# Window sums in two PSUM banks by turns, and the window's share of the first layer copied two octets ahead

## The chip, the cores and the metric

The kernel runs on one core of one Trainium2 chip. The metric is device time in microseconds (us), the median of several executions. A core has five engines that run side by side, each with its own queue of instructions: TensorE (PE in the profile; PEld is its weight load), VectorE (DVE), ScalarE (ACT), GpSimd (POOL), and SyncE (SP), which issues transfers (DMAs). They wait for each other through semaphores only. Matmul results land in PSUM, which has eight banks per partition; a bank holds 512 float32 values.

## What is computed

One layer of a graph network over 12,500 nodes with 64 features and 400,000 edges, which come sorted by `dst`, followed by a residual and a layer norm:

```python
m_in = concatenate([x[src], x[dst], edge_attr], axis=-1)      # 64 + 64 + 16
h = silu(m_in @ W1 + b1)
messages = silu(h @ W2 + b2)
agg = segment_sum(messages, dst, num_segments=12500)
z = silu(concatenate([x, agg], axis=-1) @ W3 + b3)
out = layernorm(x + z)
```

All of it is float32. Call the three 64- or 16-row parts of `W1` W1a (for `x[src]`), W1b (for `x[dst]`) and W1c (for the edge's own attributes).

## The kernel before, in words

**Tiling.** Edges are taken 128 at a time (a tile) and eight tiles make an octet: 1,024 edges. There are 391 octets (`NO`). The body of the loop over `o` (lines 610 to 681) is written out by hand for PE, ScalarE, VectorE and SyncE: `tc.manual_schedule` (line 607) keeps each engine's instructions in the order of the text. GpSimd's queue holds gathers only and runs ahead on its own.

**x[src].** At the start ScalarE writes `x @ W1a` to a table `pa` in memory (`table`, octets 1 to 7). The first 12 octets (`RAW`) gather rows of `x` itself, which TensorE transposes (line 454) and multiplies by W1a. From octet 12 on, GpSimd's `gather` (line 373) fetches the rows `pa[src]` of an octet with one indirect transfer per tile, into one of five buffers `ga`; a buffer is free again when TensorE's matmuls of line 463 have read it. Two or four tiles of some octets are not gathered: ScalarE and VectorE together move 136 columns of `x` an octet (36 and 32 each, `columns`, lines 295 to 309), one 4-byte column per instruction and at an address that a register holds, and SyncE fetches 16 rows an octet (`rows`, line 333). So most octets have eight or six gathers.

**x[dst].** As the edges are sorted, an octet's destinations lie in a window of 48 nodes (`S`). `window_load(o)` (SyncE, line 401) fetches the 48 rows of `x` twice over into `xr`; `window_product(o)` (TensorE, line 406) multiplies them by W1b into a PSUM tile of the pool `mis`; `window_copy(o)` (VectorE, line 411) multiplies that by a mask and puts it into `xw[o % 3]`, above the rows of W1c. `compare_dst(o)` (VectorE, line 433) makes the one-hot matrix `oh` that picks each edge's window row.

**An octet through the engines.** `first_layer(o)`: line 450 multiplies `xw` by `oh` into the PSUM tile `p1`; lines 460 and 463 add the columns' and the gathered parts; ScalarE moves its 36 columns and then does the silu of line 467 into `h`. `second_layer(o)`: lines 476 and 478 make `p2`, ScalarE moves its 32 columns and does the silu of line 482 into `m`. `add_up(o)` (line 491) multiplies `m` by the one-hot matrix `eh` (VectorE, line 439), which gives the sums of the window's 48 nodes; `add_window(o)` (VectorE, line 496) adds them into `agg` at an address from a register. The sums of four octets share one PSUM tile, and so one bank (`sums`, line 371).

**The order within iteration o** (what the change touches):

- TensorE: `window_product(o + 1)`, `first_layer(o)`, `add_up(o - 2)`, `second_layer(o - 1)`, then what `todo` holds.
- VectorE: `add_window(o - 4)`, `compare_dst(o + 1)`, 36 columns, `window_copy(o + 1)`, `compare_nodes(o + 1)`, 32 columns, then addresses and what `todo` holds.
- ScalarE: 36 columns, silu of `first_layer(o)`, 32 columns, silu of `second_layer(o - 1)`.
- SyncE: the transfers of octets ahead, `window_load(o + 3)`, and last the 16 rows.

**Nodes.** When no more edges can reach a group of 512 nodes, `todo` puts its output work into the loop: `node_product` (TensorE, lines 523 to 526, reads `agg`), a silu (ScalarE, line 532), and the layer norm on VectorE. Of 25 groups 23 come within the loop, one about every 16 octets; the last two come at its end.

**PSUM.** Eight banks: two for `mis` (window products, the tables, the raw octets' transposes, the node products), one for constants (`wps`), two each for `p1` and `p2`, one for the sums.

Of the kernel before, what the change touches and what calls it, by code (L numbers as in the profile page):

```python
# [9 lines left out]
F32 = mybir.dt.float32  # L10
# [4 lines left out]
OP = mybir.AluOpType  # L15
AX = mybir.AxisListType
PSUM = bass.MemoryType.PSUM
DRAM = bass.MemoryType.DRAM
ENG = mybir.EngineType

P = 128
G = 4
CT = 24
OT = 8
S = 48
# [72 lines left out]
def windows(ctx, tc, ident, badi, pa, x, xt, src_c, src_row, dst_c, dst_row, attr_t, dst_2, attr_2, base, w1, b1, w2, b2, w3, b3, out, edges):  # L98
    nc = tc.nc
# [69 lines left out]
    zero = const.tile([P, 1], F32, name="zero")  # L169
    nc.vector.memset(zero, 0.0)  # L170

    mis = ctx.enter_context(tc.tile_pool(name="mis", bufs=2, space=PSUM))


    def table(c):
        n = min(8 * P, N - c)
        ps = mis.tile([P, 8, D], F32, name="mm")
        k = (n + P - 1) // P
        for i in range(k):
            o = c + i * P  # L180
            nc.tensor.matmul(ps[:, i, :], xs[0:D, o:o + P], w1ab[:, 0, :], start=True, stop=True)
        j = c // (8 * P) % RB
        t = v[:, 2 * j:2 * j + 2].rearrange("p a i d -> p (a i) d")
        nc.scalar.copy(t[:, :k], ps[:, :k])
        f = n // P
        if f:
            nc.scalar.dma_start(pa[c:c + f * P, :].rearrange("(i p) d -> p i d", p=P), t[:, :f])
        if n % P:
            nc.scalar.dma_start(pa[c + f * P:c + n, :], t[:n % P, f, :])
# [43 lines left out]
    w1bb = fast.tile([D, 2, D], F32, name="w1bb")  # L233
    nc.vector.tensor_copy(w1bb, w1ab[:, 1:2, :].to_broadcast([D, 2, D]))
    xw = []
    for k in range(3):
        t = fast.tile([P, P], F32, name=f"xw{k}")
        nc.vector.memset(t, 0.0)
        for q in range(2):
            nc.sync.dma_start(t[E + q * A:E + (q + 1) * A, q * D:(q + 1) * D], w1[2 * D:2 * D + A, :])  # L240
        xw.append(t)
# [6 lines left out]
    with tc.tile_pool(name="gat", bufs=AHEAD + 2) as gat, tc.tile_pool(name="drp", bufs=2) as drp, \  # L248
# [2 lines left out]
            tc.tile_pool(name="work", bufs=2) as work, tc.tile_pool(name="win", bufs=3) as win, \  # L251
            tc.tile_pool(name="ps1", bufs=2, space=PSUM) as ps1, \
            tc.tile_pool(name="ps2", bufs=2, space=PSUM) as ps2, \
            tc.tile_pool(name="psa", bufs=1, space=PSUM) as psa, \
            tc.tile_pool(name="cx", bufs=4) as cx, tc.tile_pool(name="cxi", bufs=3) as cxi, \
            tc.tile_pool(name="rx", bufs=2) as rx, tc.tile_pool(name="rxi", bufs=2) as rxi, \
            tc.tile_pool(name="nx", bufs=2) as nx, tc.tile_pool(name="nv", bufs=1) as nv:
# [110 lines left out]
                    nc.vector.tensor_scalar(t[:, h], t[:, h], 4.0, float(XBASE[s] + XADDR), op0=OP.mult, op1=OP.add)  # L368

        winrow, winreg = {}, {}  # L370
        sums = psa.tile([P, 4, S], F32, name="pg")

        def gather(o):
            c, t0, n, first, last = octs[o]
# [12 lines left out]
        def bases(eng, o):  # L387

            n = min(4, NO - o)
            _, regs = nc.values_load_multi_w_load_instructions(  # L390
                bi[0:1, o:o + n], engines=(eng,), min_val=0, max_val=N - 1,
                skip_runtime_bounds_check_because="dst names a node")
            for i in range(n):
                winreg[eng, o + i] = regs[i]

        def window_load(o):
            if o % 4 == 0:
                bases(ENG.SP, o)
            xr = win.tile([D, 2, S], F32, name="xr")
            frm = xt[:, ds(winreg.pop((ENG.SP, o)), S)]  # L400
            nc.sync.dma_start(xr, frm[:, None, :].to_broadcast([D, 2, S]))
            winrow[o] = xr

        def window_product(o):
            pw = mis.tile([P, P], F32, name="mm")
            nc.tensor.matmul(pw[:E, :], winrow[o].rearrange("k s w -> k (s w)"), w1bb.rearrange("k s m -> k (s m)"),  # L406
                             start=True, stop=True)
            winrow[o] = pw

        def window_copy(o):  # L410
            nc.vector.tensor_tensor(xw[o % 3][:E, :], winrow.pop(o)[:E, :], mask[:E, :], op=OP.mult)  # L411

        def load(c, o0=0, o1=CT // OT):

# [28 lines left out]
        def first_layer(o):  # L443
            c, t0, n, first, last = octs[o]
            n2 = n + n % 2
            k = n2 // 2
            ga = got.pop(o)
            oh, eh = hots.pop(o)
            p1 = ps1.tile([P, OT // 2, P], F32, name="p1")
            nc.tensor.matmul(p1[:, :k], xw[o % 3], oh, start=True, stop=False, skip_group_check=True)  # L450
            if o < RAW:
                pt = mis.tile([P, OT // 2, P], F32, name="mm")
                for i in range(k):
                    nc.tensor.matmul(pt[:, i, :], ga[:, 2 * i:2 * i + 2, :].rearrange("p s d -> p (s d)"), ident,
                                     start=True, stop=True)
                xg = work.tile([P, OT // 2, P], F32, name="m")
                nc.vector.tensor_copy(xg[:, :k], pt[:, :k])
                nc.tensor.matmul(p1[:, :k], w1d, xg[:, :k], start=False, stop=True, skip_group_check=True)
            if o in pairs:
                nc.tensor.matmul(p1[:, 0, :], w1d, cols.pop(o), start=False, stop=False, skip_group_check=True)  # L460
            for i in range(1 if o in pairs else 0, k if o >= RAW else 0):
                g2 = single.pop(o) if o in rpairs and i == 1 else ga[:, 2 * i:2 * i + 2, :]
                nc.tensor.matmul(p1[:, i, :], g2.rearrange("p s d -> p (s d)"), ident,  # L463
                                 start=False, stop=(i == k - 1), skip_group_check=True)
            columns(o, ENG.Activation, 0)
            h = work.tile([P, OT // 2, P], F32, name="h")
            nc.scalar.activation(h[:, :k], p1[:, :k], AF.Silu, bias=b1s)  # L467
            made[o] = h, eh

        def second_layer(o):  # L470
            c, t0, n, first, last = octs[o]
            n2 = n + n % 2
            k = n2 // 2
            h, eh = made.pop(o)
            p2 = ps2.tile([P, OT, D], F32, name="p2")
            nc.tensor.matmul(p2[:, :n2, :], one3, b2r[:, :n2, :], start=True, stop=False, skip_group_check=True)  # L476
            for i in range(k):
                nc.tensor.matmul(p2[:, 2 * i:2 * i + 2, :].rearrange("p s d -> p (s d)"), h[:, i, :], w2d,  # L478
                                 start=False, stop=(i == k - 1), skip_group_check=True)
            columns(o + 1, ENG.Activation, 1)  # L480
            m = work.tile([P, OT, D], F32, name="m")
            nc.scalar.activation(m[:, :n2], p2[:, :n2], AF.Silu)  # L482
            made[o] = m, eh

        def add_up(o):
            c, t0, n, first, last = octs[o]
            m, eh = made.pop(o)
            pg = sums[:, o % 4, :]
            for i in range(n):
                s = i % 2  # L490
                nc.tensor.matmul(pg[s * D:(s + 1) * D, :], m[:, i, :], eh[:, i, :],  # L491
                                 start=(i < 2), stop=(i >= n - 2), skip_group_check=True)

        def add_window(o):
            a = agg[:, ds(winreg.pop((ENG.DVE, o)), S)]
            nc.vector.tensor_tensor(a, a, sums[:, o % 4, :], op=OP.add)  # L496


        groups = [(c, min(G * P, N - c)) for c in range(0, N, G * P)]
# [16 lines left out]
        def node_product(q):  # L516
            c, n = groups[q]
            p = n // G
            assert p * G == n
            po = mis.tile([P, G, D], F32, name="mm")  # L520
            av = agg[:, c:c + n].rearrange("k (p i) -> k i p", i=G)
            xv = xs[0:D, c:c + n].rearrange("k (p i) -> k i p", i=G)
            nc.tensor.matmul(po[:p], ones[:, :p], b3r, start=True, stop=False, skip_group_check=True)  # L523
            for i in range(G):
                nc.tensor.matmul(po[:p, i, :], xv[:, i], w3x, start=False, stop=False, skip_group_check=True)  # L525
                nc.tensor.matmul(po[:p, i, :], av[:, i], w3s, start=False, stop=(i == G - 1), skip_group_check=True)  # L526
            nodes[q].append(po)
# [62 lines left out]

        for o in range(min(AHEAD, NO)):
            gather(o)
        window_load(0)
        window_product(0)
        window_copy(0)
        load(0, 0, 1)
        load(0, 1, 3)
        window_load(1)
        window_load(2)
        relative(0, CT)  # L600
        lims = nv.tile([P, 2, LP], F32, name="lims")
        tables = list(range(0, N, 8 * P))
# [4 lines left out]
        with tc.manual_schedule(engines={ENG.PE, ENG.Activation, ENG.DVE, ENG.SP}):  # L607
            compare_dst(0)
            compare_nodes(0)
            for o in range(NO + 1):  # L610
# [27 lines left out]
                    gather(o + AHEAD)  # L638
                if o + 2 < NO and octs[o + 2][3] and o + 2:
                    load(octs[o + 2][0])  # L640
                if o + 3 < NO:
                    window_load(o + 3)
                if o + 1 < NO:
                    window_product(o + 1)
                if o % 4 == 2:
                    bases(ENG.DVE, o - 2)
                if o >= 4:
                    add_window(o - 4)
                if o + 1 < NO:
                    compare_dst(o + 1)  # L650
                columns(o, ENG.DVE, 0)
# [1 line left out]
                    first_layer(o)  # L653
                if o == 0:
                    nc.vector.tensor_copy(b2r, b2p[:, None, :].to_broadcast([3, OT, D]))
                if o + 1 < NO:
                    window_copy(o + 1)
                    compare_nodes(o + 1)
                columns(o, ENG.DVE, 1)
                if o == 1:  # L660
# [12 lines left out]
                    add_up(o - 2)  # L673
                if o >= 1:
                    second_layer(o - 1)
                address(o + 2)
                raddress(o + 2)
                rows(o)
# [21 lines left out]
        nc.vector.tensor_copy(badi, bs)  # L700

        add_up(NO - 1)
        for o in range(NO - 3, NO):
            add_window(o)
        for f, a in todo.get(NO, []):
            f(*a)
# [267 lines left out]
```

## Time and profile before

| | us |
|---|---|
| median of 3 runs (5423.18 to 5434.05) | 5430.6 |
| the profiled execution, one of the three | 5434.05 |
| its span, first to last instruction | 5432.3 |
| GpSimd, 2,585 gathers of line 382: busy | 2442.4 |
| ScalarE, 25,500 column copies of line 309: busy | 2739.9 |
| VectorE, 25,444 column copies of line 307: busy | 2071.9 |
| TensorE: matmuls busy | 2910.2 |
| first matmul of line 450 in octet 12 | 219.34 |
| first matmul of line 450 in octet 390 (the last) | 5404.21 |

So the loop takes 5185 us from octet 12 to octet 390, 13.7 us an octet. Busy time is the union of an engine's instructions; the copies overlap each other in the pipeline, so that 8 copies of 0.15 us each take 0.62 us. "Idle before" a group is how long its engine did nothing just ahead of it, and the name behind the arrow is what ended that: another engine's instruction, a DMA, or "issue" when the profile shows nothing that was waited for.

### The profile page before, as it was taken

What the parts mean: (1) busy time and instruction counts of PE and PEld (TensorE: products, weight loads), DVE (VectorE), ACT (ScalarE), POOL (GpSimd) and SP (SyncE); (2) the same over time, 40 slices, a digit from 0 to 9 for tenths busy, and PEclk for the clock granted to TensorE, in tenths of its full rate; (3) what the DMA queues carried; (4) which work ended last, traced back from release to release, by engine and by line L of the source; (5) the groups of instructions that cost most, each with busy time, mean ns of one, the idle gap of its engine ahead of it and who ended that gap; (6) DMA issues with size and microseconds to landing.
All of it is one profiled execution on the core that took longest, in us unless ns stands there. A gap on an engine that the chain in (4) does not pass through costs nothing. (4 is left out here: it accounts for less than half of the span.)

```text
span 5432.3 us, 114104 instructions
## 1 busy us (share of the span) xinstructions
PE 2910.2 (54%) x15131; PEld 2055.6 (38%) x15131; DVE 2796.6 (51%) x27841; ACT 3234.0 (60%) x26342; POOL 2535.3 (47%) x2690
## 2 busy tenths in 40 slices
PE   5654555555555455554554555555545455455556
PEld 3433333333333344333333333333433334333334
DVE  1355555555555555555555555555555555555554
ACT  1265666566565665666666656666666566666665
POOL 5544444444444444444444444444444444444443
PEclk7665656666656656666666656666566666666666
DMA  4321112111211121112112111111211121121121
GB/s 92 73 43 37 38 38 43 39 37 38 44 40 41 38 44 38 38 39 42 39 38 47 40 38 42 41 38 38 45 37 38 42 45 38 38 44 37 38 44 39
DMA packets 202940, 229.30 MB, mean 42 GB/s; under 512 B 133085, under 2 KB 141478, under 8 KB 201270
## 3 DMA queue, kind: packets, MB, share of 16 engines
q1 hardware_dynamic: 101562, 122.63, 10.1%
q0 software_dynamic: 85792, 88.02, 8.5%
q10 hardware_dynamic: 14812, 11.26, 0.9%
q14 instruction: 646, 5.29, 0.3%
q8 instruction: 128, 2.10, 0.2%
HBM read 215.26 MB, written 6.40 MB: 41 GB/s over the span
## 5 line engine op out<-in xcount | busy, mean ns | idle before, releaser
L382 POOL DMA_INDIRECT ga<-pa,sc x2585 | 2442.4, 945 | 2784.2 <-PE p L463 2059.9
L309 ACT COPY cx<-xs 64x4 uint8 x25500 | 2739.9, 188 | 1416.2 <-issue 1363.4
L307 DVE TENSOR_REDUCE cx<-xs 64x4 uint8 x25444 | 2071.9, 148 | 1817.0 <-issue 1748.0
L450 PE MATMUL p<-oh,xw 128*128 128x512 f32 (+1 forms) x782 | 793.5, 1117 | 2034.9 <-DVE xw L411 1390.2
L450 PEld LDWEIGHTS p<-oh,xw 128*128 128x128 f32 x782 | 192.2, 305 | 2140.5 <-DVE xw L411 1455.1
L463 PEld LDWEIGHTS p<-ident,ga 128*128 128x128 f32 x2586 | 597.9, 323 | 181.5 <-issue 181.2
L478 PE MATMUL p<-w2d,h 128*128 128x128 f32 x3126 | 606.8, 353 | 1.1 <-issue 1.1
L463 PE MATMUL p<-ident,ga 128*128 128x128 f32 x2586 | 600.8, 405 | 0.0
L478 PEld LDWEIGHTS p<-w2d,h 128*128 128x128 f32 x3126 | 513.7, 249 | 125.2 <-issue 125.2
L482 ACT ACTIVATE m<-p 128x512 f32<-128x512 f32 x391 | 232.3, 594 | 500.7 <-remote 408.0
L491 PE MATMUL pg<-eh,m 128*64 128x48 f32 x6250 | 352.8, 271 | 304.8 <-DVE agg L496 166.4
L491 PEld LDWEIGHTS pg<-eh,m 128*64 128x64 f32 x6250 | 304.9, 184 | 398.0 <-issue 251.4
L467 ACT ACTIVATE h<-p,b1s 128x512 f32<-128x512 f32 x391 | 267.0, 683 | 195.3 <-remote 68.5
L411 DVE TENSOR_TENSOR xw<-mm,mask 96x128 f32<-96x128 f32 x391 | 110.8, 283 | 523.6 <-issue 481.3
L406 PE MATMUL mm<-w1bb,xr 64*96 64x128 f32 x782 | 234.5, 391 | 100.3 <-remote 44.9
L433 DVE TENSOR_TENSOR oh<-dr,wrow 96x512 f32<-96x512 int32 x391 | 263.4, 674 | 3.2 <-DMA dr<-in_dst 1.8
L439 DVE TENSOR_TENSOR eh<-wrow,dc 128x384 f32<-128x384 f32 x391 | 213.4, 546 | 47.4 <-issue 47.4
L460 PEld LDWEIGHTS p<-cx,w1d 128*128 128x128 f32 x398 | 132.1, 332 | 202.2 <-issue 202.2
L406 PEld LDWEIGHTS mm<-w1bb,xr 64*96 64x96 f32 x782 | 124.3, 208 | 169.3 <-issue 57.9
L476 PE MATMUL p<-b2r,one 3*128 3x512 bf16 x391 | 186.6, 477 | 0.0
L496 DVE TENSOR_TENSOR agg<-agg,pg 128x48 f32 x391 | 77.4, 198 | 111.0 <-remote 20.5
L460 PE MATMUL p<-cx,w1d 128*128 128x128 f32 x398 | 124.7, 416 | 0.0
(81 smaller groups left out, 778.6 us busy)
## 6 DMA issues: line engine op xcount, KB each, us to landing
rx<-pa SPq DMA_DIRECT2D x5888, 0.2 KB
dr<-in_dst SPq DMA_DIRECT2D x260, 288.0 KB
ga<-pa,sc POOLq DMA_INDIRECT x2585
oh<-in_attr SPq DMA_DIRECT2D x130, 192.0 KB
xr<-in_xt SPq DMA_DIRECT2D x391, 24.0 KB
xs<-in_xt ACTq DMA_DIRECT2D x12, 512.0 KB
cxi<-in_src_row SPq DMA_DIRECT2D x199, 1.0 KB
pa<-v ACTq DMA_DIRECT2D x12, 256.0 KB
```

Source lines behind the costliest of these rows:

```text
L307: nc.vector.tensor_reduce(to, frm[:, :, None], AX.X, OP.max)
L309: nc.scalar.copy(to, frm)
L382: nc.gpsimd.indirect_dma_start(out=ga[:, i, :], out_offset=None, in_=x if o < RAW else pa[:, :], in_offset=bass.IndirectOffsetOnAxis(ap=sc ...
L406: nc.tensor.matmul(pw[:E, :], winrow[o].rearrange("k s w -> k (s w)"), w1bb.rearrange("k s m -> k (s m)"), start=True, stop=True)
L433: nc.vector.tensor_tensor(oh[:E, :], dr[:, e:e + w], wn[:E, o:o + 1].to_broadcast([E, w]), op=OP.is_equal)
L450: nc.tensor.matmul(p1[:, :k], xw[o % 3], oh, start=True, stop=False, skip_group_check=True)
L460: nc.tensor.matmul(p1[:, 0, :], w1d, cols.pop(o), start=False, stop=False, skip_group_check=True)
L463: nc.tensor.matmul(p1[:, i, :], g2.rearrange("p s d -> p (s d)"), ident, start=False, stop=(i == k - 1), skip_group_check=True)
L467: nc.scalar.activation(h[:, :k], p1[:, :k], AF.Silu, bias=b1s)
L478: nc.tensor.matmul(p2[:, 2 * i:2 * i + 2, :].rearrange("p s d -> p (s d)"), h[:, i, :], w2d, start=False, stop=(i == k - 1), skip_group_ch ...
L482: nc.scalar.activation(m[:, :n2], p2[:, :n2], AF.Silu)
L491: nc.tensor.matmul(pg[s * D:(s + 1) * D, :], m[:, i, :], eh[:, i, :], start=(i < 2), stop=(i >= n - 2), skip_group_check=True)
```

## The change

- The window product is made three octets ahead and no longer at the head of the iteration but after the second layer's matmuls; its copy goes into one of four buffers `xw`, two octets ahead; the window's load is four octets ahead.
- The pool `mis` has one PSUM buffer in place of two. The tables and the node products use `p2`'s tiles, the raw octets' transposes `p1`'s.
- The sums of an octet have a PSUM tile of their own, in two banks by turns, and `add_window` follows three octets behind in place of four.
- Before the loop, four window loads, three products and two copies come ahead of the first octet's other loads.

```diff
-    mis = ctx.enter_context(tc.tile_pool(name="mis", bufs=2, space=PSUM))
+    mis = ctx.enter_context(tc.tile_pool(name="mis", bufs=1, space=PSUM))
...
-        ps = mis.tile([P, 8, D], F32, name="mm")
+        ps = ps2.tile([P, OT, D], F32, name="p2")
...
-            tc.tile_pool(name="psa", bufs=1, space=PSUM) as psa, \
+            tc.tile_pool(name="psa", bufs=2, space=PSUM) as psa, \
...
-            nc.vector.tensor_tensor(xw[o % 3][:E, :], winrow.pop(o)[:E, :], mask[:E, :], op=OP.mult)
+            nc.vector.tensor_tensor(xw[o % 4][:E, :], winrow.pop(o)[:E, :], mask[:E, :], op=OP.mult)
...
-                pt = mis.tile([P, OT // 2, P], F32, name="mm")
+                pt = ps1.tile([P, OT // 2, P], F32, name="p1")
...
-            pg = sums[:, o % 4, :]
+            pg = sums[o] = psa.tile([P, S], F32, name="pg")
...
-            po = mis.tile([P, G, D], F32, name="mm")
+            po = ps2.tile([P, OT, D], F32, name="p2")[:, :G]
...
-        window_load(0)
-        window_product(0)
-        window_copy(0)
+        for o in range(4):
+            window_load(o)
+        for o in range(2):
+            window_product(o)
+            window_copy(o)
+        window_product(2)
         load(0, 0, 1)
         load(0, 1, 3)
-        window_load(1)
-        window_load(2)
...
-                if o + 3 < NO:
-                    window_load(o + 3)
-                if o + 1 < NO:
-                    window_product(o + 1)
-                if o % 4 == 2:
-                    bases(ENG.DVE, o - 2)
-                if o >= 4:
-                    add_window(o - 4)
+                if o + 4 < NO:
+                    window_load(o + 4)
+                if o % 4 == 1:
+                    bases(ENG.DVE, o - 1)
+                if o >= 3:
+                    add_window(o - 3)
...
+                if o + 2 < NO:
+                    window_copy(o + 2)
                 if o + 1 < NO:
-                    window_copy(o + 1)
                     compare_nodes(o + 1)
...
                 if o >= 1:
                     second_layer(o - 1)
+                if o + 3 < NO:
+                    window_product(o + 3)
                 address(o + 2)
                 raddress(o + 2)
                 rows(o)
```

More of the change, by code (lines that the diff above doesn't have):

```diff
@@ L235, in windows @@
     xw = []
-    for k in range(3):
+    for k in range(4):
         t = fast.tile([P, P], F32, name=f"xw{k}")
@@ L370, in windows @@
         winrow, winreg = {}, {}
-        sums = psa.tile([P, 4, S], F32, name="pg")
+        sums = {}
         def gather(o):
@@ L449, in first_layer @@
             p1 = ps1.tile([P, OT // 2, P], F32, name="p1")
-            nc.tensor.matmul(p1[:, :k], xw[o % 3], oh, start=True, stop=False, skip_group_check=True)
+            nc.tensor.matmul(p1[:, :k], xw[o % 4], oh, start=True, stop=False, skip_group_check=True)
             if o < RAW:
-                pt = mis.tile([P, OT // 2, P], F32, name="mm")
+                pt = ps1.tile([P, OT // 2, P], F32, name="p1")
                 for i in range(k):
@@ L495, in add_window @@
             a = agg[:, ds(winreg.pop((ENG.DVE, o)), S)]
-            nc.vector.tensor_tensor(a, a, sums[:, o % 4, :], op=OP.add)
+            nc.vector.tensor_tensor(a, a, sums.pop(o), op=OP.add)
         groups = [(c, min(G * P, N - c)) for c in range(0, N, G * P)]
@@ L702, in windows @@
         add_up(NO - 1)
-        for o in range(NO - 3, NO):
+        for o in range(NO - 2, NO):
             add_window(o)
```

## The prediction, made before the result was known

> **What bounds the kernel now.** I first read the waits, longest first in total (who waited, for whom: us in total, times, longest).
>
> ```profile
> POOL ga L382 <- PE p L463: 2059.9, 361, 10.3
> DVE cx L307 <- issue: 1748.0, 3447, 5.1
> ...
> PE p L450 <- DVE xw L411: 1390.2, 234, 9.7
> ACT cx L309 <- issue: 1363.4, 2102, 5.7
> ...
> DVE xw L411 <- issue: 481.3, 226, 6.6
> ...
> PE pg L491 <- DVE agg L496: 166.4, 175, 7.7
> ```
>
> GpSimd waits for TensorE (a free `ga` buffer), TensorE waits for VectorE's mask copy L411 and, less, for its `agg` sum L496. VectorE waits for nobody: 2796.6 busy (page, part 1) plus 1748.0 and 481.3 of "issue" is 5026 of 5432 us, and all idle time before L496 is 111.0. So the queue of VectorE sets the pace, and the question is what its "issue" time is. For that I took the busy time in four neighbouring stretches of the middle of the run (each stretch's length, then busy us and instructions by engine, granted PE clock, DMA share, GB/s).
>
> ```profile
> core 0: us, PE busy (x) PEld busy (x) DVE busy (x) ACT busy (x) POOL busy (x), PEclk, DMA share, GB/s
> 2512.00:2521.00 9.00, 0.66 (x5) 0.33 (x3) 2.03 (x20) 2.25 (x14) 5.63 (x6) 0.71 0.13 26
> 2521.00:2529.00 8.00, 6.50 (x37) 4.59 (x37) 6.13 (x67) 7.71 (x70) 2.83 (x3) 0.69 0.48 112
> 2529.00:2534.00 5.00, 0.00 (x0) 0.00 (x0) 0.97 (x8) 1.36 (x9) 2.83 (x3) 0.54 0.18 34
> 2534.00:2542.00 8.00, 6.78 (x37) 4.73 (x37) 6.17 (x64) 7.87 (x71) 2.83 (x3) 0.65 0.06 12
> ```
>
> The chip runs in two modes: eight us in which VectorE does 64 to 67 instructions and ScalarE 70, then five to nine in which they do 8 to 20 and 9 to 14. The timeline shows the slow mode close by (start, length, engine, line; idle before).
>
> ```profile
> 2518.14 0.19 ACT L309 COPY cx<-xs 64x4 uint8 x1 [1.17 <-issue]
> 2518.15 0.15 DVE L307 TENSOR_REDUCE cx<-xs 64x4 uint8 x1 [1.25 <-issue]
> ...
> 2518.84 0.19 ACT L309 COPY cx<-xs 64x4 uint8 x1 [0.51 <-issue]
> 2518.85 0.15 DVE L307 TENSOR_REDUCE cx<-xs 64x4 uint8 x1 [0.55 <-issue]
> ...
> 2521.04 0.27 DVE L411 TENSOR_TENSOR xw<-mm,mask 96x128 f32<-96x128 f32 x1
> ...
> 2521.36 0.50 PEld L450 LDWEIGHTS p<-oh,xw 128*128 128x128 f32 x2 [8.91 <-DVE xw L411]
> ```
>
> Both engines start one or two instructions together about every 0.7 us; GpSimd's gathers go on. I call it a silence. From the starts of all instructions of PE, DVE, ACT and SP I worked out: 2,560 gaps over 0.45 us, 1857 us together, a third of the span. Silences belong to gathers. Of the bursts of eight (168, 9.7 us long) the first silence comes 4.2 us after the first gather, the last ends 1.6 us after the last, 6.4 us are silent; of the bursts of six (168, 7.2 us) the numbers are 4.3, 1.2 and 3.7. The idle time ahead of a burst (2 to 9 us) makes a microsecond of difference at most. So an octet is a ring: L411 ends; L450 starts (mean 0.9 us later); L463 ends 3.7 later; the burst starts 0.3 later; silence 4.2 later. VectorE has some 9.3 us of work an octet (2796.6 / 391 = 7.15 busy, and about 2.1 of register loads between eights of copies), so silence catches it just short of the next L411: the median has 6 copies left. L411 comes before the silence in 5% of the bursts, within it in 36%, after it in 59%. The mean octet (20 to 369) is 13.83 us = VectorE's work, plus silence, less what gets through in it (mean 5.6 copies and 0.7 other instructions).
>
> **The change part by part.**
>
> *Sums in two banks, add_window an octet earlier.* L491 no longer waits for L496 (166.4 us on TensorE). This is worth 0: TensorE stands idle 2034.9 us before L450 (part 5), which hides it. What is late next is `m`: L491 now starts 3.0 us (mean) after it, in 5% of octets under 1.2. L496 needs the sums of an octet ago, with a whole octet to spare; VectorE issues the same number of each kind of instruction. If ScalarE fell behind by the 3 us, TensorE's idle time would take it.
>
> *The copy two octets ahead.* L450 of octet o+1 needs the copy of the iteration before. But in the changed order L406 of octet o+3 stands right ahead of it in TensorE's queue, and with one buffer in `mis` L406 waits until L411 of iteration o has read the product before: the same L411 that L450 waits for now. The wait moves from L450 to L406 and nothing is decoupled. L406 joins the path: from its start to L450's 0.66 us (2398.26 to 2398.92 in the next fence). Behind it wait L450, L463 and so GpSimd. Price in two ways. If the ring set the pace wherever L411 comes in or after silence: 0.66 x 0.95 x 365 octets in silence's reach = +229 us, the upper end. If VectorE uses the 0.66 us to finish its six copies (6 x 0.067 + one load of 0.3 = 0.7) so that L411 and L439 no longer wait for the silence's end: -0.66 x 0.59 x 365 = -142 us, the lower end. VectorE's row (no waits) is the nearest, so by itself the delay costs 0; what is left is which instructions fall into silence. L411 and L439 take 0.22 + 0.54 us of VectorE's time and pass in two steps of 0.7, in which else 1.5 copies (0.15 us) pass: 0.6 us gained where they move in. That is half of the 59%, 108 octets, 65 us; half of the 36% move out at its front, 66 octets, 39 us. I take -26.
>
> *Node products.* This I looked for because they share TensorE's queue. Here is octet 168's (L450 in the last line is octet 169's):
>
> ```profile
> 2391.85 1.22 PE L523 MATMUL mm<-b3r,ones 1*128 1x256 f32 x2
> ...
> 2394.12 0.28 DVE L411 TENSOR_TENSOR xw<-mm,mask 96x128 f32<-96x128 f32 x1
> ...
> 2397.60 0.73 PE L526 MATMUL mm<-w3s,agg 128*128 128x64 f32 x2
> ...
> 2398.26 0.74 PE L406 MATMUL mm<-w1bb,xr 64*96 64x128 f32 x2
> ...
> 2398.36 0.20 DVE L496 TENSOR_TENSOR agg<-agg,pg 128x48 f32 x1 [0.26 <-PE mm L526]
> ...
> 2398.92 2.07 PE L450 MATMUL p<-oh,xw 128*128 128x512 f32 x2
> ```
>
> A node product takes 5.9 us (mean of 23), and VectorE's next L496 waits for its end, as it writes the `agg` that L526 reads. It now starts 4.9 us ahead of L411 (mean) and is over in time. After the change it stands behind the waiting L406: it starts 0.29 + 0.05 + 0.66 = 1.0 us after L411's start and ends at 6.9. VectorE reaches L496 3.9 us after L411 in 16 of the 23, later in the others. Taking each one's own numbers, the waits sum to 50 us; 3 are there already: +47, on the engine that sets the pace. Ends: 0 if they all fall into silence; +104 (23 x 4.5, L450's added delay) if the ring counts. The first of all, octet 24's at 393 us, shows the case already: its product started 0.35 us after L411, and L496 stood 2.56 us. ScalarE's silu L532 behind it also waits; its cover is ScalarE's slack, some 0.8 us an octet by its gaps outside silences, and TensorE's idle time.
>
> *Start and end.* More loads come ahead of octet 0, and `p1` is shared with the transposes for 12 octets; octet 0 may start up to 5 us earlier, while the gathers of the first octets run in one burst to 62 us anyway. Value 0, ends -20 and +20. At the end one sum fewer: -0.2.
>
> Sum: 5434.05 - 26 + 47 = 5455. The profiled run is 3.4 above the median: **5452 us**, +0.4%.
>
> **A rule of the skill.** In the silences ScalarE stands still with VectorE: its copies, 0.09 us apart at 2521, are 0.7 apart at 2518. The Trainium skill, "SBUF — State Buffer", section "SBUF: two separate sides", says that only VectorE and GpSimd can block each other and that TensorE and ScalarE never wait on anyone. By it a silence would stop VectorE alone and never hold L450 behind it, so that the -26 falls away: 5478. The trace differs, and I go by it.
>
> **Rivals.** *Faster: the silence swallows the mask copy.* The 65 us of gain come without the loss at the front, and the node products fall half into silences: 5431 - 65 + 23 = 5389, and with more of the -142 down to 5330. For it: six copies left is almost exactly 0.66 us. Against: VectorE's work is the same, so the ring can lock a few copies further on. *Slower: TensorE's ring sets the pace.* If VectorE gets to L411 ahead of TensorE, the 0.66 us count in full in half the octets, +115, which with the +47 gives 5593; in a quarter of them, 5536. It decides from the point where L411 itself stands idle for L406. Against: there is a whole octet of room. *No effect.* The wait only moves to L406, silences and the two prices cancel: within 0.2% (about what a measurement of this kernel can tell from no change), 5431.
>
> **How the numbers follow.** Forecast (5442 to 5500) 0.40; faster rival 0.31; slower rival 0.16; no effect 0.13. Slower 0.56, same 0.13, faster 0.31. The range leaves out a tenth at each side: it cuts the faster rival at 5360 and the slower at 5560.
>
> **What would show it.** Right: PE's wait for L411 stands before L406, of the same size as now before L450; L491's wait for L496 is gone; some 20 waits of L496 for L526 of 2 to 3 us; 1800 to 1900 us of silence; median copies left at its start under 3. Wrong: L450 starts without L406 waiting for L411; bursts that join (more silence per gather); idle time before L411 that ends with L406; octets 12 to 390 in another time than 5185 + 21 us, or the start to octet 12 off by more than 20.

## The result and the profile after

The changed kernel takes **5481.0 us** (median of 4 executions, 5470.4 to 5491.5) against 5427.9 us for the kernel before, measured beside it (4 executions, 5423.2 to 5434.1): a ratio of 1.0097 [1.0074, 1.0120]. The forecast was 5452, slower by 0.4%; it is slower by 1.0%. The profiled execution took 5479.6 us, with a span of 5477.8, 45.5 us more than before.

The waits of the changed kernel (who waited, for whom: us in total, times, longest):

```profile
POOL ga L382 <- PE p L463: 2034.4, 328, 16.6
DVE cx L307 <- issue: 1801.0, 3424, 5.5
...
PE mm L406 <- DVE xw L411: 1278.5, 194, 10.5
...
DVE xw L411 <- issue: 393.6, 161, 6.2
...
PE pg L491 <- ACT m L482: 332.4, 105, 15.7
...
DVE agg L496 <- PE p L526: 71.8, 23, 7.6
```

TensorE's 1390.2 us of waiting for the mask copy L411 have not gone. They stand one product further up, before L406, at 1278.5. The wait of L491 for VectorE's L496 (166.4) is gone, and a wait of L491 for ScalarE's `m` has come (332.4). New on VectorE is the last line: 23 waits of L496 for the node product, one for each node product in the loop. The waits of the kernel before had these lines for the two pairs that grew:

```profile
PE pg L491 <- ACT m L482: 31.5, 16, 7.9
...
DVE agg L496 <- PE mm L526: 2.8, 2, 2.6
```

The groups of page part 5 say the same of L406 and L450 (busy us, mean ns of one; idle before it, what ended most of it). First the changed kernel:

```profile
L406 PE MATMUL mm<-w1bb,xr 64*96 64x128 f32 x782 | 277.5, 455 | 2050.0 <-DVE xw L411 1278.5
L450 PE MATMUL p<-oh,xw 128*128 128x512 f32 (+1 forms) x782 | 773.1, 1090 | 5.3 <-DMA oh<-in_attr 5.3
```

Then the kernel before:

```profile
L450 PE MATMUL p<-oh,xw 128*128 128x512 f32 (+1 forms) x782 | 793.5, 1117 | 2034.9 <-DVE xw L411 1390.2
```

Before, the 2034.9 us of idle time were L450's. Now L450 has 5.3 of them, and L406 has 2050.0. Octet 168's node product shows the whole chain; it is the one that the prediction showed in the profile of before (timeline: start, length, engine, line; idle before):

```profile
2401.00 0.27 DVE L411 TENSOR_TENSOR xw<-mm,mask 96x128 f32<-96x128 f32 x1
...
2401.32 0.74 PE L406 MATMUL mm<-w1bb,xr 64*96 64x128 f32 x2 [4.13 <-DVE xw L411]
...
2401.99 1.22 PE L523 MATMUL p<-b3r,ones 1*128 1x256 f32 x2
...
2407.74 0.73 PE L526 MATMUL p<-w3s,agg 128*128 128x64 f32 x2
...
2408.26 2.02 PE L450 MATMUL p<-oh,xw 128*128 128x512 f32 x2
...
2408.50 0.20 DVE L496 TENSOR_TENSOR agg<-agg,pg 128x48 f32 x1 [4.02 <-PE p L526]
```

The mask copy starts at 2401.00, and only then does L406 get through. Behind it comes the node product, whose last piece ends at 2408.47, and VectorE, the engine that sets the pace, stands for 4.02 us before L496. In the kernel before the same product had begun at 2391.85, ahead of the copy, and L496 stood for 0.26.

Where the 45.5 us are, cut at the starts of L433 on VectorE (once an octet):

| | before | after | difference |
|---|---|---|---|
| start, to octet 13's L433 | 220.9 | 214.3 | -6.6 |
| 138 octets: six from each of the 23 node products on | 1866.1 | 1958.0 | +91.9 |
| the other 239 octets | 3311.8 | 3273.2 | -38.6 |
| from the last L433 to the end | 33.5 | 32.3 | -1.2 |

With eight octets from each product instead of six, the two middle rows are +82.3 and -29.0, so the border between them is soft by some 10 us; and each column is a single trace, of kernels whose executions lie 11 us (before) and 21 us (after) apart. Silences (gaps over 0.45 us between starts of PE, DVE, ACT and SP) sum to 1813 us, before 1857.

### The profile page after: what moved, and what is told of

Its sections match the earlier page's. It is cut to its first block, busy times and chain, and to the rows that moved or that the text cites. A ratio compares the mean times of both kernels' runs of the same rounds, so it can differ in the third digit from the quotient of the medians.

```text
span 5477.8 us, 114041 instructions
## 1 busy us (share of the span) xinstructions
PE 2888.0 (53%) x15131; PEld 2033.1 (37%) x15131; DVE 2793.3 (51%) x27842; ACT 3226.0 (59%) x26342; POOL 2532.0 (46%) x2690
## 5 line engine op out<-in xcount | busy, mean ns | idle before, releaser
L406 PE MATMUL mm<-w1bb,xr 64*96 64x128 f32 x782 | 277.5, 455 | 2050.0 <-DVE xw L411 1278.5
L406 PEld LDWEIGHTS mm<-w1bb,xr 64*96 64x96 f32 x782 | 147.2, 245 | 2139.9 <-DVE xw L411 1332.1
L450 PE MATMUL p<-oh,xw 128*128 128x512 f32 (+1 forms) x782 | 773.1, 1090 | 5.3 <-DMA oh<-in_attr 5.3
L463 PEld LDWEIGHTS p<-ident,ga 128*128 128x128 f32 x2586 | 569.5, 309 | 174.0 <-issue 170.1
L491 PE MATMUL pg<-eh,m 128*64 128x48 f32 x6250 | 356.5, 275 | 451.4 <-ACT m L482 332.4
L463 PE MATMUL p<-ident,ga 128*128 128x128 f32 x2586 | 571.2, 390 | 0.0
L491 PEld LDWEIGHTS pg<-eh,m 128*64 128x64 f32 x6250 | 301.3, 186 | 536.6 <-ACT m L482 364.7
L411 DVE TENSOR_TENSOR xw<-mm,mask 96x128 f32<-96x128 f32 x391 | 110.3, 282 | 453.5 <-issue 393.6
L433 DVE TENSOR_TENSOR oh<-dr,wrow 96x512 f32<-96x512 int32 x391 | 263.5, 674 | 12.4 <-DMA dr<-in_dst 12.3
L450 PEld LDWEIGHTS p<-oh,xw 128*128 128x128 f32 x782 | 188.7, 300 | 101.8 <-issue 94.3
L496 DVE TENSOR_TENSOR agg<-agg,pg 128x48 f32 x391 | 77.3, 198 | 182.7 <-PE p L526 71.8
```

Source lines behind the costliest of these rows:

```text
L433: nc.vector.tensor_tensor(oh[:E, :], dr[:, e:e + w], wn[:E, o:o + 1].to_broadcast([E, w]), op=OP.is_equal)
L450: nc.tensor.matmul(p1[:, :k], xw[o % 4], oh, start=True, stop=False, skip_group_check=True)
```

## The experiments

**The silences belong to the chip or the occasion, not to the program.** The experiments ran on three chips, numbers 7, 4 and 3; the number of the chip of the comparison above is not on record. On these three the kernel before, the same program, took 3575.4, 3578.6 and 3576.6 us (medians of 29, 16 and 19 executions, all between 3563.8 and 3585.0), and no kernel that was traced there had more than 50 us of silences. 5432 less the 1857 us of silence is 3575; for the changed kernel the same sum, 5478 less 1813, gives 3665, where its trace without silences took 3614, so the first agreement is partly chance. What makes the silences is not settled; no run with silences came again. So each ratio below is to the kernel before on the same chip, and what the change does within silences rests on the first two traces alone. Where an expectation speaks of times near 5400, it was written for a chip with silences.

**Node products ahead of the waiting product.** The changed kernel, with what `todo` holds put ahead of L406:

```
-                if o + 3 < NO:
-                    window_product(o + 3)
...
                     for f, a in todo.get(o, []):
                         f(*a)
+                if o + 3 < NO:
+                    window_product(o + 3)
```

> The changed kernel with one line moved: in each iteration the window product L406 comes after the node products, not ahead of them, so that a node product no longer stands behind the waiting L406. Theory A (VectorE's queue plus the silences set the pace; the change loses its time at the 23 node octets, where the six octets around a node product take 85.13 us in place of 81.14, 92 us in all, while the other octets gain 0.17 us each): the 92 us go, the gain stays, so about 5390 us (5370 to 5410), ratio to before 0.993, with waits of VectorE's L496 for L526 near 0. Rival B (the 0.66 us of L406 on the path to each gather burst is the loss, 391 octets): the time stays near 5480, ratio 1.01.

Measured: 3568.5 us, ratio 0.9987 [0.9974, 1.0000]. L496 waits 9.6 us for L526, in 7 places instead of 23 (`DVE agg L496 <- PE p L526: 9.6, 7, 2.3`). The expected gain (0.993) was meant for a chip with silences. Without them, moving these few instructions of TensorE, and nothing else, takes the loss away that the changed kernel has there (1.0113, below).

**ScalarE's silu an octet later.** `node_silu` (L532) stands behind the node product too; here it is put off by an octet (`later(o + 1, node_silu, q)` in place of `later(o, node_silu, q)`), so that ScalarE does not stand for it.

> The changed kernel with ScalarE's node silu (L532) one octet later; TensorE's order and VectorE's wait at L496 stay as they are. It splits the 92 us of the node octets. If VectorE's wait alone (72 us by the profile) is the price: same as the changed kernel, 5480 us. If ScalarE's wait (92 us before L532) and what follows from it (TensorE waiting 332 us for ScalarE's m at L491) adds to it: 20 to 45 us less, 5435 to 5460.

Measured: 3617.3 us, ratio 1.0117 [1.0099, 1.0134]. From the waits of this kernel:

```profile
DVE agg L496 <- PE p L526: 67.9, 23, 3.6
...
ACT z L532 <- PE p L526: 9.9, 2, 7.1
```

ScalarE's wait is gone (it was 161.4 us in the changed kernel without silences), VectorE's is as it was, and the loss is still there. ScalarE's wait is not on the path.

**One bank, two products.** The changed kernel with the sums in one bank of four again, and the bank that this frees given to `mis`: its copy two octets ahead is now really free of the copy before it.

```
-    mis = ctx.enter_context(tc.tile_pool(name="mis", bufs=1, space=PSUM))
+    mis = ctx.enter_context(tc.tile_pool(name="mis", bufs=2, space=PSUM))
...
-            tc.tile_pool(name="psa", bufs=2, space=PSUM) as psa, \
+            tc.tile_pool(name="psa", bufs=1, space=PSUM) as psa, \
...
-        sums = {}
+        sums = psa.tile([P, 4, S], F32, name="pg")
...
```

> The changed kernel with the sums of four octets in one PSUM bank again and two buffers in mis: now L406 waits for no copy of its own iteration, and L450 is really free of L411 of the same iteration; in exchange L491 waits for L496 again. Theory A (VectorE's queue plus silences): VectorE's work is the same, so the time stays within 60 us of before (5370 to 5490), although L450 starts some 3 us earlier against L411. Rival B (the ring through TensorE and GpSimd sets the pace): 3 us less an octet, down by 300 us or more, until GpSimd's 10 us an octet show. Rival C (gather bursts that start earlier join, and silences grow): slower by over 100 us, more silence per gather than 0.69 us.

Measured: 3579.1 us, ratio 1.0011 [1.0000, 1.0023]. From its waits:

```profile
PE pg L491 <- DVE agg L496: 885.9, 294, 6.7
...
DVE agg L496 <- PE p L526: 31.3, 16, 2.6
```

L406 waits for L411 no longer (0.4 us in all), the node products find their way past, and the loss is gone again. TensorE now spends 885.9 us before L491 on VectorE's L496, and that costs nothing: idle time of TensorE is not what sets the end.

**First matmul twice.** In the kernel before, the matmul of L450 issued twice: a longer way on TensorE from L411 to L463, in every octet.

```
             nc.tensor.matmul(p1[:, :k], xw[o % 3], oh, start=True, stop=False, skip_group_check=True)
+            nc.tensor.matmul(p1[:, :k], xw[o % 3], oh, start=True, stop=False, skip_group_check=True)
```

> The kernel before with the matmul L450 issued twice in each octet (the second overwrites the first), which puts 2.07 us more on the path from L411 to the gather burst, 391 times. Theory A (VectorE's queue plus silences set the pace): within 80 us of before, because VectorE uses the 2 us to run ahead before the next silence. Rival B (the ring sets the pace): +570 to +810 us, 6000 to 6240 us.

Measured: 3563.3 us, ratio 0.9975 [0.9961, 0.9988]. The edit puts 391 times two pieces of 0.77 us (median) on TensorE, some 600 us in all, but the way grew by less: the granted clock rose from 0.73 in the trace of before to 0.83, the other matmuls took less time, and TensorE's busy time went from 2647.1 to 2740.6 us only. From the start of L411 to the end of L463 an octet took 4.66 us in place of 3.97 (means of octets 20 to 369). If the ring set the pace, these 0.69 us would cost some 270 us in 391 octets; the kernel is not slower at all. The third experiment says the same from the other side: there L450 starts 8.7 us (mean) after its copy and waits for it no longer, and the time stays. So the rival "TensorE's ring sets the pace" falls, without silences.

**The changed kernel again**, unchanged, for a trace without silences.

> The changed kernel itself, beside the kernels below. In the first four experiments the kernel before took 3575 us, with no silences in the profile, so the change has to be measured there too. Theory A' (VectorE's queue sets the pace; what the change costs is VectorE's 23 waits of 3 us at L496 for L526, and nothing else without silences): 68 us of waits, less some 8 us that are there before, so +45 to +65 us, ratio 1.013 to 1.018, and the same as with the node silu one octet later (1.0117), as ScalarE is not on the path. Rival (the silences made the loss): ratio 1.000 without silences. If silences are there again: 1.0097 as in the first measurement.

Measured: 3621.0 us, ratio 1.0113 [1.0097, 1.0128]. In microseconds that is 42 more than before, against 53 in the first comparison, which had silences. It is under the expected 1.013 to 1.018, because the wait that was taken as some 8 us before the change is 25.5 there (see the kernel before again, below). Its waits:

```profile
PE mm L406 <- DVE xw L411: 826.5, 338, 5.8
...
ACT z L532 <- PE p L526: 161.4, 25, 8.0
...
DVE agg L496 <- PE p L526: 66.5, 23, 3.6
```

**Node products twice.** The changed kernel with the matmuls of a node product issued twice, so that each is some six microseconds longer. (The first pass is overwritten by the second.)

```
-            nc.tensor.matmul(po[:p], ones[:, :p], b3r, start=True, stop=False, skip_group_check=True)
...
+            for _ in range(2):
+                nc.tensor.matmul(po[:p], ones[:, :p], b3r, start=True, stop=False, skip_group_check=True)
...
```

> The changed kernel with the matmuls of every node product issued twice, the second over the first (6.2 us more behind the waiting L406, 23 times in the loop). Theory A': VectorE's waits at L496 grow from 3 to some 9 us each, +130 to +145 us over the changed kernel. Rival (TensorE's slack takes it, the wait at L496 is a symptom): within 20 us of the changed kernel.

Measured: 3777.5 us, ratio 1.0552 [1.0536, 1.0568]. Its waits (the lines behind 523 stand one lower, so L527 is L526):

```profile
DVE agg L496 <- PE p L527: 217.0, 23, 10.0
```

150.5 us more of this wait than in the changed kernel, and 156.5 us more time, somewhat over the +130 to +145 that were expected. In the traces 150.1 us of it are in the octets behind the node products and 9.7 at the end, where the last two products are doubled too. A microsecond of this wait is a microsecond of the kernel, which TensorE's work in the fourth experiment was not.

**Sums in two banks alone.** The kernel before with the sums by turns, `add_window(o - 3)` and the pools of the changed kernel, but with the copy one octet ahead and the window product at the head of the iteration.

```
-        sums = psa.tile([P, 4, S], F32, name="pg")
+        sums = {}
...
-                if o >= 4:
-                    add_window(o - 4)
+                if o >= 3:
+                    add_window(o - 3)
```

> The kernel before with the PSUM part of the change alone: sums in two banks by turns, add_window three octets behind, one buffer in mis, tables and node products in p2's tiles; the window product stays at the head of the iteration and its copy one octet ahead. L406 waits for L411 as in the changed kernel, but the node products stand ahead of it. Theory A': as with the nodes ahead, ratio 0.995 to 1.001. Rival (the sums' new place or the one buffer in mis costs the time): as the changed kernel, 1.01 or more.

Measured: 3568.7 us, ratio 0.9975 [0.9965, 0.9985]; L496 waits 19.5 us for L526 in 11 places. The half of the change that has to do with the sums costs nothing; the loss is the other half's.

**Two products, and node products ahead.** The first and the third experiment together: `todo` ahead of L406, sums in one bank, two buffers in `mis`.

> The changed kernel with one bank for the sums, two buffers in mis, and the node products ahead of the window product: no L406 waits for the copy of its iteration and no node product stands behind a wait of that kind. With the node products behind L406 this kernel had 31 us of waits at L496 for L526 and a ratio of 1.001. Theory A': those 31 us go, ratio 0.990 to 0.996, below every kernel so far. Rival (VectorE's waits at L496 are not additive): 0.998 to 1.002.

Measured: 3566.8 us, ratio 0.9968 [0.9956, 0.9980]; L496's wait 21.7 us in 15 places. It beats both kernels, by 0.3% and by some 1.4%, but the expected 0.990 to 0.996 was missed: two thirds of the wait of the third experiment (31.3) are still there. TensorE's wait before L491 for L496 is 885.7 us here, as large as in the third experiment, and worth as little.

**The kernel before again**, for its trace without silences, **and the first experiment again**, on the third chip.

> The kernel before, unchanged, for a trace of it on this occasion. If this chip shows none of the silences (gaps over 0.45 us below 50 us in all), both theories expect about 3575 us and 8.85 us an octet away from the node octets, as in every kernel traced there; the inherited-wait theory expects six octets around a node octet at 55.5 to 56.7 us (the changed kernel had 58.1), L496's waits for L526 below 35 us, and TensorE's wait for L411 before L450, not before L406. The rival, that the change also costs something in every octet, expects octets away from the nodes at 8.83 or less. If this chip shows silences, 5430 us and 1850 us of silence.

> The changed kernel with the window product moved behind what the node list holds, as tried before, on another occasion. Without silences: 0.997 to 1.000 of the kernel before, 55.7 us for six octets around a node octet. With silences: if the whole loss there was the node products' too, the six octets fall from 85.1 us to about 81 and the time to some 5390 (5481 less 23 x 4.0); the rival, that silences make the moved wait dear by itself, leaves it above 5430.

Measured: 3571.6 us for the kernel before, 0.9996 [0.9984, 1.0007] to itself, and 3569.0 us, 0.9977 [0.9964, 0.9989], with the node products ahead. The six octets take 56.5 us in the first and 56.1 in the second, 58.1 in the changed kernel; octets away from node products (of octets 20 to 369) take 8.87, 8.86 and 8.85 us. The waits of the kernel before, without silences:

```profile
PE pg L491 <- DVE agg L496: 401.4, 293, 4.8
...
PE p L450 <- DVE xw L411: 389.9, 281, 2.6
...
DVE agg L496 <- PE mm L526: 25.5, 15, 6.6
```

The wait that decides is there before the change too, at 25.5 us. The next view, four stretches of 9 us in the middle of the same run (each stretch, then busy us and instructions by engine, granted PE clock, DMA share, GB/s), shows what is missing on this chip:

```profile
1800.00:1809.00 9.00, 6.31 (x32) 4.24 (x33) 6.83 (x77) 8.40 (x74) 6.80 (x8) 0.66 0.57 117
1809.00:1818.00 9.00, 6.00 (x43) 4.75 (x42) 7.16 (x77) 8.79 (x80) 6.62 (x8) 0.88 0.17 31
1818.00:1827.00 9.00, 7.68 (x38) 5.63 (x36) 6.60 (x74) 4.88 (x37) 6.86 (x8) 0.50 0.29 64
1827.00:1836.00 9.00, 9.00 (x47) 6.62 (x47) 6.30 (x65) 5.87 (x51) 3.09 (x4) 0.63 0.41 87
```

GpSimd issues eight gathers in a stretch, and VectorE starts 65 to 77 instructions beside them; in the prediction's first silent stretch it started 20 beside six. VectorE's 2667.8 us busy and 649.5 of "issue" fill 3317 of the 3572.6.

**One number for ten kernels.** From each trace without silences: the wait of L496 for the node product, and the time of the 138 octets around node products.

| kernel | wait, us | 138 octets, us | difference |
|---|---|---|---|
| first matmul twice | 3.6 | 1276.5 | 1272.9 |
| node products ahead | 9.6 | 1280.2 | 1270.6 |
| node products ahead, again | 19.0 | 1289.7 | 1270.7 |
| sums alone | 19.5 | 1290.9 | 1271.4 |
| two products, nodes ahead | 21.7 | 1292.3 | 1270.6 |
| before | 25.5 | 1299.7 | 1274.2 |
| one bank, two products | 31.3 | 1301.3 | 1270.0 |
| changed | 66.5 | 1336.7 | 1270.2 |
| changed, silu later | 67.9 | 1338.0 | 1270.1 |
| node products twice | 217.0 | 1486.8 | 1269.8 |

The wait spans 213 us, the remainder 4.4. The other 239 octets take 2102.8 to 2111.9 us; the two kernels with the order of before are the longest there (2111.9, and 2109.5 with the first matmul doubled) as they are in the remainder, so the changed orders gain up to some 10 us that the wait does not explain. But without silences this wait is nearly the whole difference in the loop. What it does not explain either is the start: octet 13's L433 starts at 127.6 us in the trace of before and at 142.3 to 146.9 in all others, the doubled first matmul among them, whose start is the code of before. So it is taken for the spread of one execution, and nothing is read from it; no second trace of before tests that. It does not leave the sums of single traces alone: the changed kernel's trace is 41.6 us longer than that of before, of which +37.0 are in the 138 octets, -9.0 in the others, +14.7 at the start and -1.1 at the end.

## Why the prediction was right, and which term was small

The direction and the mechanism are those that the prediction gave. The size was off: its terms added up to +21 us, and octets 12 to 390 took 5237.2 us, 52.4 more than before and not 21, which the prediction itself had named as a sign against it. One term makes up most of that, the node products.

**VectorE's queue sets the pace: right,** shown without silences: a way on TensorE that is 0.69 us longer in every octet cost nothing, 150.5 us of waits before VectorE's L496 cost 156.5. VectorE's work was put too high, at 9.3 us an octet: without silences its busy time and its "issue" come to 8.5 (3317 / 391), in an octet of 8.85.

**The wait moves from L450 to L406: right,** 1390.2 before the one, 1278.5 before the other.

**Sums in two banks, worth 0: right** by time without silences (0.9975 alone; 885.7 us of L491's wait in the best version). What was late next was not quite as written: L491 started 3.0 us (mean) after `m` before and now starts 1.5 us after it, with 332.4 us of waiting for it. The prediction named what covers this, TensorE's idle time. Without silences the changed kernel waits 26.1 us for `m`.

**Silences, -26: right in sign and near in size** (-38.6 or -29.0 in the other octets), in part by luck: the route was only half the one named, and 9.0 us of gain in these octets stand between the traces without silences too. L411 came ahead of a burst's silence in 15% of the bursts (before 5%), within in 36% (36%) and after in 48% (59%): about a tenth of the bursts moved in and as many out, where the prediction moved three in ten in and almost two in ten out. The median copies left were 4, not under 3. More copies got through a silence, 7.4 on average against 5.6. That part was not tested by experiment, and no run shows how much of the gain it made.

**Start 0: right within its bounds** (-6.6). **End -0.2:** -1.2.

**Node products, +47: the term that was mis-sized.** The waits themselves measured +69 (71.8 less 2.8), the octets behind the products +91.9 over six and +82.3 over eight. The mechanism is the one given: 23 waits, on VectorE, for a product behind the waiting L406. The geometry holds where there are no silences: the prediction had the node product start 1.0 us after L411, end at 6.9, and VectorE reach L496 at 3.9; without silences the means are 0.84, 7.01 and 4.2, and the wait grows by 41.0 us (25.5 to 66.5) as the 138 octets grow by 37.0. Within silences the means are 2.46, 8.85 and 5.8: in nine of the 23 the product started 3.2 to 5.6 us after L411, and it lasted 6.38 us where the trace of before gave 5.91. So a wait was 3.1 us on average and not the 2.2 of the prediction's sum. The last 13 to 23 us, on top of the waits themselves, are in the octets that follow; late gathers that then fall badly into silences are a guess that no run here tests.

The Trainium skill, "TensorE: Matmul & The Clock Gate", Part 2, says that only weight loads are pulled ahead and that matmuls stay in program order. On the order of the matmuls the trace agrees: behind an L406 that waits 4.13 us, L523 starts at 2401.99, after it, and the timeline shows nothing else that it waited for.

**The rivals.** "The silence swallows the mask copy" went wrong in size: the gain was there, 29 to 39 us and not 65, but the node products did not fall into silences. "TensorE's ring" is refuted without silences and left open within them. "No effect" is outside the interval of the ratio. The prediction also held the silences against what the Trainium skill says of SBUF ports; no run shows that a silence is a wait at such a port, so they neither support nor contradict that page.

## What to carry to other kernels

A buffer more on one side of a wait decouples nothing if the instruction that fills it needs a pool of one: the wait goes to the new head of the queue, and everything behind it in the text inherits it, the rare work too. So when an instruction that waits is moved in a hand-written order, list what now stands behind it and ask of each whether the engine that sets the pace waits for it; putting 23 rare products ahead of it was worth 1.3% here, without silences. A kernel's bound is found by doubling: waits on the bound's path cost their full length, work off it nothing. Read from the trace what a doubling really added: 600 us of matmuls made TensorE's busy time 93.5 us longer here.

## What the runs showed of the chip that was not expected

- The same program took 5428 us in the first comparison and 3575 to 3579 us on the three chips of the experiments. The traces differ by the silences (1857 us against under 50). Ratios of the change agree nevertheless, 1.0097 [1.0074, 1.0120] and 1.0113 [1.0097, 1.0128], though in microseconds they are 53 and 42.
- More work on TensorE raised its granted clock: 0.83 on average with the first matmul doubled, 0.73 in the trace of before without silences. The Trainium skill, "TensorE: Matmul & The Clock Gate", Part 1, says that the default is throttled and that activity releases the throttle; this pair agrees. With it L496's wait for the node product fell from 25.5 to 3.6 us; that the clock did this was not tested by itself. Added work is not the only thing that raises the clock: it was 0.76 to 0.77 with two products (third and eighth experiment), where TensorE runs the same matmuls.
